# Attention in a fused block kernel: query and key stacks padded with zeros to all 128 rows

## The chip, the cores and the metric

The kernel runs on one core of a Trainium2 chip, in one launch. The metric is the device time of that launch in microseconds (us), as the median of several runs; less is better. A further execution is recorded by the hardware profiler. Engines are named as in the profile: PE multiplies matrices (PEld is its weight load), DVE, ACT and POOL work on vectors, SP issues most of the DMA transfers. "PEclk" is the share of its full clock that TensorE was granted. L1104 is line 1104 of the kernel before.

## What is computed

Four sequences of 512 tokens with 128 channels pass through four residual blocks: a Mamba block with a mixture of eight experts, a feed-forward block (FFN), causal attention with 16 heads of 8 channels, and the same FFN again. Attention is the part that the change touches:

```python
q = (x @ W_dq.T @ W_uq.T).reshape(B, T, nh, hs)
q_lat = jnp.einsum('bqhd,hdl->bhql', q, k_eff)
attn = jnp.einsum('bhql,bkl->bhqk', q_lat, c_kv) / sqrt(hs)
attn = jnp.where(causal[None, None], attn, -jnp.inf)
attn = jax.nn.softmax(attn, axis=-1)
y_lat = jnp.einsum('bhqk,bkl->bhql', attn, c_kv)
y = jnp.einsum('bhql,hld->bqhd', y_lat, v_eff).reshape(B, T, C)
```

## The kernel before

The first half of the launch runs the Mamba scan of one sequence after another, with routing, experts and FFN of earlier sequences beside it. The second half is attention, again beside what is left of experts, FFN and projections.

**Stacks.** The projection of a sequence (`project`, L500 to L533) splits each fp32 query and key value into three bf16 parts and stores them in DRAM (`q_d` at L528, three copies in `k_d` at L531, both issued by POOL). Attention goes by eight units, a unit being eight heads of a sequence. `fill(u)` (L1079) loads a unit into one of three pairs of stacks, `qs` and `ks`, with six DMAs on SP's queue. A stack has 96 rows: rows 0 to 71 (`NP9`) hold three blocks of 24 rows, arranged so that one bf16 matmul over 72 rows sums the nine products of the parts. Rows 72 to 74 of `ks` hold -1 for good (`below`, written once per stack by the DMA of L1062); rows 72 to 74 of `qs` receive the three bf16 parts of the row maxima.

**Maxima.** `maxima(u)` (L1090) computes all scores of a unit over rows 0 to 71 (L1104), adds the causal mask on the diagonal block by a 128-row matmul with the identity (L1108), and DVE takes the row maximum straight from PSUM (L1100). The maxima are split (L1120 to L1123), transposed (L1127), written to DRAM (`m_d`, L1133) and read back into three rows of `qs` (L1134), both by POOL.

**Exponentials.** `exps(G)` (L1140) takes four heads: it computes the transposed scores over 75 rows (L1157), in which the three extra rows subtract the maximum, adds the mask (L1165), and ACT takes the exponential (L1170). `weigh(G)` (L1173) multiplies the exponentials with the values in fp32, four heads side by side of 32 columns each (`po`, L1184), and transposes the result (L1198).

Per four heads `exps` streams 5,120 columns of scores and 2,048 of masks; `maxima` streams 10,240 and 4,096 per unit.

**Order.** The loop at L1254 interleaves the exponentials of one half unit, the maxima of the next unit, the weighing of the half unit before, and pieces of the experts (L335 to L391), the FFN (L426 to L459) and the projections. Python emits that order, and in this second half a scheduler of the framework then sets each engine's final order by its own estimates of durations, so an edit can move instructions that it does not name. PSUM tiles of scores are double (`sq`, `st`), the general tile `mm` is single.

Of the kernel before, what the change touches and what calls it, by code (L numbers as in the profile page):

```python
# [10 lines left out]
BF16 = mybir.dt.bfloat16  # L11
# [5 lines left out]
P = 128  # L17
B, L, C = 4, 512, 128
# [7 lines left out]
NH, HS, KVL = 16, 8, 64  # L26
# [11 lines left out]
def block_kernel(ctx, tc, x, rms1_w, rms2_w, in_proj_w, conv_w, conv_b, x_proj_w,  # L38
                 dt_proj_w, dt_proj_b, A_log, D_skip, out_proj_w, router_w, Wg, Wu, Wd,
                 W_dq, W_dqT, W_uqT, W_dkvT, W_uk, W_uv, W_oT, w_gateT, w_upT, w_downT, out):  # L40
    nc = tc.nc
    const = ctx.enter_context(tc.tile_pool(name="const", bufs=1))
# [45 lines left out]

    below = const.tile([3, L], BF16, tag="below", name="below")
    nc.gpsimd.memset(below, -1.0)  # L90
    identb = const.tile([P, P], BF16, tag="identb", name="identb")
    nc.vector.tensor_copy(identb, ident)
    maskq = const.tile([P, P], BF16, tag="maskq", name="maskq")
# [92 lines left out]
    rows = [keep.tile([P, NT, 2], I32, tag="rows", name=f"rows{b}") for b in range(B)]  # L186
# [410 lines left out]
    with ExitStack() as first:  # L597
        w1 = first.enter_context(tc.tile_pool(name="s1", bufs=1))
# [6 lines left out]
        h0, xi, sz, dt, bc, c_d, delta, du = {}, {}, {}, {}, {}, {}, {}, {}  # L605
# [430 lines left out]
    with ExitStack() as second:  # L1036
        def pool(name, bufs, **more):
            return second.enter_context(
                tc.tile_pool(name=name, bufs=bufs, reuse_waits="tile", **more)
            )  # L1040

        w1, w2 = pool("a1", 1), pool("a2", 2)
# [9 lines left out]

        NP9 = 9 * HS
        NU = NH // 2
        UNITS = 2 * B
        qs, ks = [], []
        for i in range(3):
            qs.append(w1.tile([96, NU, L], BF16, tag=f"qs{i}", name=f"qs{i}"))  # L1060
            k = w1.tile([96, NU, L], BF16, tag=f"ks{i}", name=f"ks{i}")
            nc.sync.dma_start(  # L1062
                k[NP9 : NP9 + 3, :, :], below.unsqueeze(1).to_broadcast([3, NU, L])
            )
            ks.append(k)

        def values(b):
            va, qk = vs[b % 2], stores[b][2]
# [10 lines left out]
        def fill(u):  # L1079

            b, h0 = u // 2, (u % 2) * NU
            q_d, k_d, _ = stores[b]
            for i in range(3):
                at = slice(3 * HS * i, 3 * HS * (i + 1))
                for stack, of in ((qs[u % 3], q_d), (ks[u % 3], k_d[i])):
                    nc.sync.dma_start(
                        stack[at], of[:, :, h0 : h0 + NU, :].rearrange("j d h l -> (j d) h l")
                    )

        def maxima(u):  # L1090

            q, k = qs[u % 3], ks[u % 3]
            mx = w2.tile([P, NT, NU], F32, tag="mx", name="mx")
            taken = None
            for t in range(NT):
                w = (t + 1) * P
                n = L // w
                for h0 in range(0, NU, n):
                    if taken:
                        nc.vector.tensor_reduce(*taken, AX.X, ALU.max)  # L1100
                    sc = ps_q.tile([P, L], F32, tag="sq", name="sc")
                    for h in range(h0, h0 + n):
                        c = (h - h0) * w
                        nc.tensor.matmul(  # L1104
                            sc[:, c : c + w], q[0:NP9, h, t * P : w], k[0:NP9, h, 0:w],
                            start=(h == h0), stop=False, skip_group_check=True,
                        )
                    nc.tensor.matmul(  # L1108
                        sc[:, 0 : n * w].rearrange("p (h k) -> p h k", k=w)[:, :, t * P : w],
                        identb, maskq.unsqueeze(1).to_broadcast([P, n, P]),  # L1110
                        start=False, stop=True, skip_group_check=True,
                    )
                    taken = (
                        mx[:, t, h0 : h0 + n], sc[:, 0 : n * w].rearrange("p (h k) -> p h k", k=w)
                    )
                    yield
            nc.vector.tensor_reduce(*taken, AX.X, ALU.max)
            parts = w2.tile([P, NT, 3, NU], BF16, tag="mparts", name="mparts")
            rest = w2.tile([P, NT, NU], F32, tag="mrest", name="mrest")
            nc.vector.tensor_copy(parts[:, :, 0, :], mx)  # L1120
            nc.vector.tensor_tensor(rest, mx, parts[:, :, 0, :], ALU.subtract)
            nc.vector.tensor_copy(parts[:, :, 1, :], rest)
            nc.vector.tensor_tensor(parts[:, :, 2, :], rest, parts[:, :, 1, :], ALU.subtract)  # L1123
            yield
            pm = ps.tile([3 * NU, L], BF16, tag="mm", name="pmx")
            for t in range(NT):
                nc.tensor.transpose(  # L1127
                    pm[:, t * P : (t + 1) * P], parts[:, t].rearrange("p i h -> p (i h)"), identb
                )
            mT = w2.tile([3 * NU, L], BF16, tag="mT", name="mT")  # L1130
            nc.scalar.copy(mT, pm)  # L1131
            m_d = dram.tile([3, NU, L], BF16, tag="m_d", name="m_d")
            nc.gpsimd.dma_start(m_d.rearrange("i h l -> (i h) l"), mT)  # L1133
            nc.gpsimd.dma_start(q[NP9 : NP9 + 3, :, :], m_d)  # L1134
            yield

        scale = float(HS) ** -0.5
# [2 lines left out]
        def exps(G):  # L1140


            u, h0 = G // 2, 4 * (G % 2)
            q, k = qs[u % 3], ks[u % 3]
            probs[G] = got = [{} for _ in range(4)]

            for blocks in (
                [(0, 0, 0)], [(1, 0, 0)], [(2, 0, 0)], [(3, 0, 0)],
                [(0, 1, 0), (0, 3, L - P)], [(1, 1, 0), (1, 3, L - P)],
                [(2, 1, 0), (2, 3, L - P)], [(3, 1, 0), (3, 3, L - P)],  # L1150
                [(0, 2, 0), (1, 2, 2 * P)], [(2, 2, 0), (3, 2, 2 * P)],
            ):
                pt = ps_t.tile([P, L], F32, tag="st", name="st")
                p = w2.tile([P, L], F32, tag="p", name="p", bufs=PBUFS)
                for j, kt, c in blocks:
                    rows = slice(kt * P, (kt + 1) * P)
                    nc.tensor.matmul(  # L1157
                        pt[:, c : c + L - kt * P], k[0 : NP9 + 3, h0 + j, rows],
                        q[0 : NP9 + 3, h0 + j, kt * P : L],
                        start=(c == 0), stop=False, skip_group_check=True,  # L1160
                    )
                    got[j][kt] = p[:, c : c + L - kt * P]

                n, step = len(blocks), blocks[-1][2] // P or 1
                nc.tensor.matmul(  # L1165
                    pt.rearrange("p (a c) -> p a c", c=P)[:, 0 : step * (n - 1) + 1 : step, :],
                    identb, maskk.unsqueeze(1).to_broadcast([P, n, P]),
                    start=False, stop=True, skip_group_check=True,
                )
                ready[G] = nc.scalar.activation(p, pt, AF.Exp, scale=scale).ins  # L1170
                yield
# [74 lines left out]
        while 0 not in stores:  # L1246
            turn(*streams)
        fill(0)
        fill(1)
        for _ in range(2):  # L1250
            turn(*streams)
        for _ in times(2, maxima(0)):
            turn(*streams)
        for G in range(2 * UNITS + 1):  # L1254
            u = G // 2
            if G % 2 == 0:
                ends.add(*(last(b) for b in begin.get(u, ())))
                while filled < min(u + 3, UNITS) and filled // 2 in stores:
                    fill(filled)
                    filled += 1  # L1260
                if u < UNITS and u % 2 == 0:
                    values(u // 2)
                while u + 1 < UNITS and filled <= u + 1:
                    turn(*streams)
                    if filled // 2 in stores:
                        fill(filled)
                        filled += 1
                more = maxima(u + 1) if u + 1 < UNITS else iter(())
            scores = exps(G) if G < 2 * UNITS else iter(())
            weighed = weigh(G - 1) if 1 <= G else iter(())  # L1270
            for step in range(10):
# [74 lines left out]
```

## Time and profile before

| what | value |
|---|---|
| median of 3 runs | 939.68 us (939.14 to 942.08) |
| the profiled execution | 941.45 us, of which its span is 939.6 us |
| mean granted clock of TensorE | 0.854 |
| PE, DVE, ACT, POOL busy | 734.1, 580.3, 411.2, 309.4 us |
| bytes moved by DMA | 99.16 MB, 106 GB/s over the span |
| first and last matmul of L1104 | 470.4 and 872.8 us from the span's start |
| first and last matmul of L1157 | 525.6 and 901.9 us |

In a group's row, "72\*128 72x384 bf16" means 72 rows and 128 columns of the array in use and a moving operand of 72 partitions by 384 elements; then follow the count, the busy time with the mean in ns of one, and the idle time of the engine just before, with what ended it. A row of a view by stretches has the stretch, its length, each engine's busy time with the number of instructions begun, the granted clock, the share of the DMA engines and their rate.

### The profile page before, as it was taken

The page shows a single profiled execution, that of the slowest core. Times are in us where ns is not written, and L with a number is a line of the kernel's source. Part 1 is how long each engine was busy: PE and PEld are TensorE (multiplying, and loading weights), DVE is VectorE, ACT ScalarE, POOL GpSimd, SP SyncE. Part 2 cuts the span into 40 slices and gives each one's busy share as a digit, 9 for nine tenths or more (in the row PEclk, how much of TensorE's full clock was granted, in tenths as well). Part 3 has the DMA queues.
Part 4 walks back from the last instruction along what each step waited for, and adds up shares of the span by engine and source line. Part 5 has one row for each costly group of instructions (what it writes and reads, how often), then busy time and mean ns, then how long its engine had stood idle before and what let it go on. Part 6 is the DMA issues. An engine that isn't in the chain of part 4 may idle for free. (4 is left out here: it accounts for less than half of the span.)

```text
span 939.6 us, 11943 instructions
## 1 busy us (share of the span) xinstructions
PE 734.1 (78%) x3763; PEld 429.0 (46%) x3763; DVE 580.3 (62%) x1151; ACT 411.2 (44%) x794; POOL 309.4 (33%) x243
## 2 busy tenths in 40 slices
PE   5386698689879865788398799789858997889854
PEld 2132243255356621557357476458724454355432
DVE  4395999899989898747274552166544156566311
ACT  2836548535854431324103354503345533554641
POOL 1153664856556348432402104000161402300010
PEclk9688789789989977799759599979968897997987
DMA  4138221163157412516546235817410330600000
GB/s 103 35 140 325 65 68 47 53 194 112 64 171 233 132 46 82 172 46 202 178 125 204 80 117 168 211 45 220 143 43 3 93 87 7 163 16 3 3 12 11
DMA packets 84480, 99.16 MB, mean 106 GB/s; under 512 B 10370, under 2 KB 56458, under 8 KB 83242
## 3 DMA queue, kind: packets, MB, share of 16 engines
q1 hardware_dynamic: 78881, 87.09, 31.3%
q0 software_dynamic: 4352, 10.89, 3.6%
q10 hardware_dynamic: 1184, 0.43, 0.2%
q8 instruction: 30, 0.49, 0.2%
q14 instruction: 33, 0.26, 0.1%
HBM read 76.67 MB, written 21.63 MB: 105 GB/s over the span
## 5 line engine op out<-in xcount | busy, mean ns | idle before, releaser
L886 POOL TENSOR_TENSOR hc<-hst,cs 128x1024 f32<-128x1024 f32 x64 | 150.6, 2353 | 138.7 <-issue 34.3
L832 PE MATMUL yp<-hc,ident 128*128 128x512 f32 x256 | 150.6, 718 | 43.6 <-POOL hc L886 42.5
L874 DVE TENSOR_TENSOR_SCAN hst<-da,bx 128x1024 f32<-128x1024 f32 x64 | 146.3, 2286 | 10.7 <-POOL hc L886 3.7
L1100 DVE TENSOR_REDUCE mx<-sc 128x1 f32<-128x384 f32 (+3 forms) x168 | 102.7, 636 | 66.4 <-PE sc L1108 64.8
L832 PEld LDWEIGHTS yp<-hc,ident 128*128 128x128 f32 x256 | 52.7, 220 | 140.6 <-POOL hc L886 98.9
L1170 ACT ACTIVATE p<-st 128x512 f32<-128x512 f32 x160 | 90.9, 598 | 34.3 <-PE st L1165 31.0
L812 ACT ACTIVATE da<-delta,A 128x512 f32<-128x512 f32 (+1 forms) x128 | 84.7, 715 | 41.1 <-DVE hst L874 38.5
L1104 PE MATMUL sc<-ks,qs 72*128 72x128 bf16 (+3 forms) x256 | 76.7, 358 | 15.5 <-DMA ks<-k_d 8.2
L854 DVE TENSOR_TENSOR bx<-du,pb 128x1024 f32<-128x1024 f32 x64 | 78.3, 1223 | 5.0 <-POOL du L803 2.5
L319 DVE SCALAR_TENSOR_TENSOR thm<-thm,mpg 128x512 f32<-128x512 f32 x53 | 36.1, 680 | 70.4 <-ACT thm L380 70.4
L374 PE MATMUL mpg<-xTm,wgu 128*128 128x128 f32 x424 | 67.1, 301 | 11.1 <-DMA wgu<-in_Wg_dram 6.7
L1157 PE MATMUL st<-qs,ks 75*128 75x512 bf16 (+3 forms) x256 | 67.7, 331 | 10.3 <-ACT p L1170 5.6
L374 PEld LDWEIGHTS mpg<-xTm,wgu 128*128 128x128 f32 x424 | 60.3, 214 | 20.3 <-issue 8.4
L374 PE MATMUL mpu<-xTm,wgu 128*128 128x128 f32 x424 | 62.2, 292 | 5.8 <-DVE mh L320 4.1
L1133 POOL DMA_DIRECT2D m_d<-mT x8 | 4.4, 550 | 184.3 <-ACT mT L1131 184.3
L367 ACT ACTIVATE xTm<-mpt,r2w 128x128 f32<-128x128 f32 x53 | 19.4, 366 | 102.9 <-PE mpt L365 102.9
L386 PE MATMUL mpd<-wd,mh 128*128 128x128 f32 x424 | 60.2, 286 | 2.8 <-ACT xTm L367 2.3
L374 PEld LDWEIGHTS mpu<-xTm,wgu 128*128 128x128 f32 x424 | 57.3, 209 | 8.7 <-DVE mh L320 4.4
L822 PE MATMUL pb<-bc,pick 96*128 96x512 bf16 x64 | 27.4, 429 | 41.8 <-DVE bx L854 38.0
L386 PEld LDWEIGHTS mpd<-wd,mh 128*128 128x128 f32 x424 | 53.4, 197 | 7.0 <-ACT xTm L367 5.3
L1108 PE MATMUL sc<-maskq,identb 128*128 128x128 bf16 (+2 forms) x176 | 50.1, 284 | 0.0
L380 ACT ACTIVATE thm<-mpg 128x512 f32<-128x512 f32 x53 | 31.7, 597 | 40.9 <-PE mpg L374 39.9
(242 smaller groups left out, 1167.1 us busy)
## 6 DMA issues: line engine op xcount, KB each, us to landing
cs<-c_d SPq DMA_DIRECT2D x64, 256.0 KB
wgu<-in_Wg_dram SPq DMA_DIRECT2D x53, 256.0 KB
wgu<-in_Wu_dram SPq DMA_DIRECT2D x53, 256.0 KB
wd<-in_Wd_dram SPq DMA_DIRECT2D x53, 256.0 KB
xg<-zero SPq DMA_DIRECT2D x8, 1024.0 KB
qs<-q_d SPq DMA_DIRECT2D x24, 192.0 KB
k_d<-parts POOLq DMA_DIRECT2D x12, 384.0 KB, 4.0
ks<-k_d SPq DMA_DIRECT2D x24, 192.0 KB
```

What stands on the lines that cost most here:

```text
L374: nc.tensor.matmul(pp[:, f, :], w[:, k, f * P : (f + 1) * P], rows_in, start=True, stop=True,)
L386: nc.tensor.matmul(pd, hT[:, f, :], w[:, f, :], start=(f == 0), stop=(f == NFC - 1))
L812: nc.scalar.activation(da[:, e, e:], delta[b][:, e, e:], AF.Exp, scale=A[:, e, n : n + 1])
L832: nc.tensor.matmul(yps[b][:, e, :], ident, hc[:, e, :], start=(n == 0), stop=(n == NS - 1))
L854: nc.vector.tensor_tensor(bxs[s], du[s // NS], taps[s][1].unsqueeze(1).to_broadcast([P, NE, L]), ALU.mult)
L874: nc.vector.tensor_tensor_scan(hst.rearrange("p e l -> p (e l)"), dec.pop(s).rearrange("p e l -> p (e l)"), bxs.pop(s).rearrange("p e l -> ...
L886: done = nc.gpsimd.tensor_tensor(hc, hst, cs.unsqueeze(1).to_broadcast([P, NE, L]), ALU.mult).ins
L1100: nc.vector.tensor_reduce(*taken, AX.X, ALU.max)
L1104: nc.tensor.matmul(sc[:, c : c + w], q[0:NP9, h, t * P : w], k[0:NP9, h, 0:w], start=(h == h0), stop=False, skip_group_check=True,)
L1108: nc.tensor.matmul(sc[:, 0 : n * w].rearrange("p (h k) -> p h k", k=w)[:, :, t * P : w], identb, maskq.unsqueeze(1).to_broadcast([P, n, P] ...
L1157: nc.tensor.matmul(pt[:, c : c + L - kt * P], k[0 : NP9 + 3, h0 + j, rows], q[0 : NP9 + 3, h0 + j, kt * P : L], start=(c == 0), stop=False ...
L1170: ready[G] = nc.scalar.activation(p, pt, AF.Exp, scale=scale).ins
```

## The change

Both stacks get 128 rows. Rows 0 to 71 stay as they are, rows 72 to 124 are zeros in both, and the rows of the maxima and of -1 move to 125 to 127. The matmuls of the maxima then run over 125 rows, those of the exponentials over 128. The zeros come from a new constant `blank` of 53 partitions by 512, set once by POOL; when each of the three pairs is filled for the first time (units 0, 1 and 2), two DMAs on SP's queue copy it eight times over into `qs` and `ks` (53 x 8 x 512 bf16, 434 KB each). The DMA of `below` moves from the set-up to the same place.

```diff
+    blank = const.tile([P - 3 - 9 * HS, L], BF16, tag="blank", name="blank")
+    nc.gpsimd.memset(blank, 0.0)
...
-        NP9 = 9 * HS
+        NP9, MXR = 9 * HS, P - 3
...
-            qs.append(w1.tile([96, NU, L], BF16, tag=f"qs{i}", name=f"qs{i}"))
-            k = w1.tile([96, NU, L], BF16, tag=f"ks{i}", name=f"ks{i}")
-            nc.sync.dma_start(
-                k[NP9 : NP9 + 3, :, :], below.unsqueeze(1).to_broadcast([3, NU, L])
-            )
-            ks.append(k)
+            qs.append(w1.tile([P, NU, L], BF16, tag=f"qs{i}", name=f"qs{i}"))
+            ks.append(w1.tile([P, NU, L], BF16, tag=f"ks{i}", name=f"ks{i}"))
...
+            if u < 3:
+                for stack in (qs[u], ks[u]):
+                    nc.sync.dma_start(
+                        stack[NP9:MXR], blank.unsqueeze(1).to_broadcast([MXR - NP9, NU, L])
+                    )
+                nc.sync.dma_start(ks[u][MXR:P], below.unsqueeze(1).to_broadcast([3, NU, L]))
...
-                            sc[:, c : c + w], q[0:NP9, h, t * P : w], k[0:NP9, h, 0:w],
+                            sc[:, c : c + w], q[0:MXR, h, t * P : w], k[0:MXR, h, 0:w],
...
-            nc.gpsimd.dma_start(q[NP9 : NP9 + 3, :, :], m_d)
+            nc.gpsimd.dma_start(q[MXR:P, :, :], m_d)
...
-                        pt[:, c : c + L - kt * P], k[0 : NP9 + 3, h0 + j, rows],
-                        q[0 : NP9 + 3, h0 + j, kt * P : L],
+                        pt[:, c : c + L - kt * P], k[:, h0 + j, rows],
+                        q[:, h0 + j, kt * P : L],
```

In the built program PE, DVE and ACT have the same instructions as before, POOL has one more (the setting of `blank`) and SP six more DMAs. On SP the fills of `qs` and `ks` of unit 0 stand where the three DMAs of `below` stood; the fill of unit 1's `qs` stands just ahead of an expert's weight loads and of the first load of `q_d`; the fill of unit 1's `ks` stands between the six loads of unit 0 and those of unit 1; both fills of unit 2 stand some 80 places ahead of unit 2's loads. The scheduler also orders PE anew in two stretches: between the maxima of units 0 and 2, and in the stretch of experts beside unit 2's maxima. From the scores of the second sequence to the end PE's order is the same, but for one pair of exponential and maxima steps.

## The prediction

> **What bounds the kernel.** I read the page's slices first. From slice 20 on (470 us) attention runs, and PE is the fullest engine by far; but the clock row shows that it is often not granted its full clock while it is full.
>
> ```profile
> PE   5386698689879865788398799789858997889854
> ...
> PEclk9688789789989977799759599979968897997987
> ```
>
> So I asked for stretches of low clock with PE busy (columns: PE, PEld, DVE, ACT, POOL busy, then the clock):
>
> ```profile
> core 0: us, PE busy (x) PEld busy (x) DVE busy (x) ACT busy (x) POOL busy (x), PEclk, DMA share, GB/s
> 470.40:488.00 17.60, 16.24 (x65) 7.92 (x65) 14.61 (x27) 0.37 (x1) 0.00 (x0) 0.50 0.61 159
> 525.20:538.00 12.80, 12.80 (x55) 7.09 (x52) 7.75 (x21) 7.60 (x15) 0.00 (x0) 0.50 0.12 43
> 538.00:541.00 3.00, 3.00 (x34) 1.04 (x34) 0.20 (x1) 0.80 (x2) 0.00 (x0) 0.77 0.00 0
> 621.30:634.90 13.60, 12.72 (x52) 8.43 (x52) 9.36 (x18) 0.96 (x2) 0.00 (x0) 0.50 0.00 0
> ...
> 720.30:737.30 17.00, 15.16 (x37) 6.01 (x36) 6.18 (x49) 11.35 (x23) 2.97 (x4) 0.60 0.00 0
> 771.50:778.30 6.80, 6.04 (x21) 2.38 (x19) 5.90 (x11) 0.00 (x0) 0.00 (x0) 0.50 0.01 2
> 856.80:866.10 9.30, 9.24 (x41) 4.90 (x38) 5.95 (x16) 5.89 (x11) 1.13 (x1) 0.50 0.01 2
> 866.10:870.50 4.40, 4.40 (x33) 1.38 (x32) 2.25 (x15) 0.28 (x1) 0.00 (x0) 0.50 0.00 0
> ```
>
> From 525 to 538 us PE has no gap at all and still gets half its clock. These stretches hold the score matmuls; they end when 128-row fp32 matmuls of experts, FFN or `po` come. The next view sets two full stretches against each other, PE alone: scores and masks, then experts, and what follows the experts.
>
> ```profile
> core 0: us, PE busy (x), PEclk, DMA share, GB/s
> 529.10:532.50 3.40, 3.40 (x17) 0.50 0.01 2
> 532.50:535.90 3.40, 3.40 (x17) 0.50 0.00 0
> 631.50:634.90 3.40, 3.40 (x18) 0.50 0.00 0
> 635.00:638.40 3.40, 3.40 (x30) 1.00 0.37 101
> ```
>
> **What sets the clock.** The Trainium skill ("TensorE: Matmul & The Clock Gate", Part 1, The HAM clock gate) says that the clock follows how busy PE has been, and opens after one busy window of about 3.4 us. The changes of clock in this trace do lie on a grid of 3.41 us. But 12.80 us busy of 12.80 at clock 0.50 contradicts the rest: busy time alone is not what counts. I laid the trace's matmuls on that grid and counted streamed columns, fp32 twice, each weighted by rows in use over 128 and columns in use over 128, against what half the clock could stream. Of 80 windows at half clock, the 53 that stayed there reach at most 0.74, the 27 that opened have at least 0.75: no overlap. Without the weight by rows, a window with 1.00 stays shut and one with 0.79 opens. At full clock, the clock falls when about 0.36 of the full capacity is no longer reached (28 falls, none above 0.40; 162 stay, none under 0.33). From the code, a PE full of `exps` reaches (5120 x 75/128 + 2048) / 7168 = 0.70, full of `maxima` (10240 x 72/128 + 4096) / 14336 = 0.69: under 0.75 however full it is. After the change these are 1.00 and 0.98. The masks count in full although their identity and most of their mask are zeros (leaving them out, 3 of 80 windows go wrong), so I take zero rows to count. By the skill's rule the change gains nothing and costs what its DMAs cost; by the trace it opens the clock. I follow the trace.
>
> **The matmuls themselves.** 256 + 256 matmuls get more rows. Weight loads show no cost of rows: 115 and 108 ns with 72 and 75 rows, 108 ns with 128.
>
> ```profile
> L1104 PEld LDWEIGHTS <-qs 72*128 72x128 bf16 x256 | 27.8, 115 | 31.4 <-issue 26.4
> L1157 PEld LDWEIGHTS <-ks 75*128 75x128 bf16 x256 | 27.2, 108 | 29.0 <-issue 21.7
> L1108 PEld LDWEIGHTS <-identb 128*128 128x128 bf16 x176 | 18.9, 108 | 16.6 <-issue 12.9
> ```
>
> Matmuls at one clock are as long as their columns: nothing here.
>
> **What the clock gives, stretch by stretch.** A stretch at full clock can't be shorter than half its PE time, nor than its DVE or ACT time; nor do these overlap fully. The same sequence of steps as at 856.0 to 866.1 (10.10 us) runs at full clock in 792.8 to 800.4, 7.60 us, with ACT busy 5.93 of it (0.78) and with two projection matmuls of 1.06 us together that the other lacks. So I divide the largest of the three by about 0.85, and `po` goes from 4.43 to about 2.35 us:
>
> ```profile
> 847.96 2.29 PE po L1184 x32
> 866.17 4.43 PE po L1184 x32
> ```
>
> - 470.4 to 488 (first maxima): DVE is busy 14.61 of 17.60, so it binds (in the same loop at full clock, 616 to 620, it was busy 3.99 of 4). Up to 2.5, less the first window, cold after idle, and the start: 1. Then experts start at full clock instead of cold until 491.6: about 1. Together 2.0.
> - 525.2 to 541: the first 3.9 us stay cold after idle. The remaining 8.9 us hold 5.4 of DVE and 5.3 of ACT, over 0.85 is 6.3: 2.6; `po` 0.6. Together 3.2.
> - 621.3 to 634.9: DVE binds until 628 (0.2), then cold experts fill PE for 6.8 us: half would be 3.4, I take 2.8. Together 3.0.
> - 682.7 to 689.6, the same pattern: 0, since the FFN behind it waits for POOL's gathers of expert rows until 700 us anyway.
> - 720.3 to 737.3: ACT 11.35 / 0.85 = 13.4, so 3.6; but projection matmuls with 64 rows in it can still shut the clock: 2.5.
> - 771.5 to 778.3: DVE 5.90 binds: 0.4.
> - 856.8 to 870.5: between 9.30 - 5.95 / 0.85 = 2.3 and 10.10 - (7.60 - 1.06) = 3.6, take 2.2; `po` 2.0. Together 4.2.
>
> Sum: 15.3 us. Bounds: with DVE and ACT no limit it would be about 30; with the clock shutting again where DVE binds (there a window weighs only about 0.38 to 0.40 at full clock, close to the 0.36 of the falls), 7.
>
> **The DMAs.** Six fills of 424 packets of 1 KB. The 1 KB packets of `below` took 82 ns each, so a fill is 424 x 82 / 16 = 2.2 us of all DMA engines if spread evenly, up to twice that if not, and 0.8 to 1.4 us of SP (`below` 0.78, the zero fill of the experts' rows 1.39). Unit 0's two run in 409 to 423 us, where DMA was idle (1 GB/s at 410 to 412): 0. Unit 2's two come near 543 us, with DMA nearly idle until 555: 0. The fill of unit 1's `ks` stands behind the load that PE waits for (second row below) and ahead of unit 1's loads, not used before 492; weight loads behind it land 2.2 us later, against experts at 488: 0 to 1, take 0.5. The fill of unit 1's `qs` comes near 446 us, where ACT waits for the store of `q_d` and PE behind it (first row):
>
> ```profile
> PE mpt L365 <- ACT full L523: 7.2, 1, 7.2
> PE sc L1104 <- DMA ks<-k_d: 8.2, 1, 8.2
> ```
>
> 0 to 4.4, take 1.0, as the store is on another queue and starts at 448. The setting of `blank` on POOL costs 0.5 us at 3 us, ahead of nothing used before 11 us: 0. The moved `below` DMAs ride with the fills. The new order of PE between 492 and 600 us: -2 to +2, take 0.
>
> **Sum.** -15.3 + 1.5 = -13.8 us, against the profiled 941.45: 927.7. The median stands 1.8 under that execution: 939.7 - 13.8 = 925.9.
>
> **Rivals.** A measurement of this kernel can tell about 0.3% (2.8 us) from no change.
> - *The clock opens as said* (0.60): 925.9, own range 916 to 932.
> - *It opens, but waits take most of it* (0.18): DVE and ACT bind nearer to 1.0, and windows near 0.36 shut again. For: DVE 14.61 of 17.60 and ACT 11.35 of 17.00. Against: `po` and experts bind on PE alone, 7 us. -7 + 1.5: 934.
> - *Zero rows don't count, or a weight I took for rows is one for bf16* (0.10): the change doesn't do what it says. For: the score matmuls are also nearly the only bf16 ones; a weight of 0.7 for bf16 misplaces just 3 windows of 80. Then +1.5: 941.
> - *Slower* (0.12): the same shut clock, and the fills lie on the path: unit 1's `qs` fill holds up the store of `q_d` (4.4 if uneven) and unit 1's `ks` fill the weights at 488 (up to 2.2). It decides if the clock stays 0.50 in the first exponentials and PE's wait for `full` exceeds 9 us: 945.
>
> Faster by over 0.3%: 0.78; within: 0.10; slower: 0.12. The range runs from the 916 of the first case to 941, which takes in the second and most of the third.
>
> **What would show it.** Right: clock 1.0 from one window after the first `exps` starts, mean clock near 0.88, `po` never at 4.4 us, L1104 and L1157 means well under 358 and 331 ns, PE's wait before the first L1104 still near 8 us. Wrong: a PE full of 128-row scores at 0.50 for over two windows; or a clock that is open with the time unchanged, and DVE or ACT waits longer by as much.

## The result and the profile after

The changed kernel takes 993.05 us (median of 4 runs, 991.29 to 998.51), the kernel before 940.88 beside it: a ratio of 1.056 (95% interval 1.052 to 1.061). The profiled execution took 993.71 us with a span of 991.9. The forecast was 925.9, and 993 lies far outside its range of 916 to 941. Medians are over all runs of a kernel and ratios over those within 1.5% of its fastest, which matters for the kernel before, 938.2 over 39 runs and 934.6 over 21 in the first of the three sets below, and for `rows80`, 935.6 over 20 and 930.1 over 11.

In the changed kernel the scores are L1109, their mask L1113, the exponentials' scores L1162, `po` L1189, the experts' first product L377; the fills are L1084 (`blank`) and L1087 (`below`), the loads of the stacks L1091. Two rows of the slices and three of the groups from the page of the changed kernel, then the same three groups before:

```profile
PE   5396697699798757836356890888985887979964
...
PEclk9687798799999767868577795899997998989997
...
L377 PE MATMUL mpg<-xTm,wgu 128*128 128x128 f32 x424 | 70.2, 310 | 59.7 <-DMA wgu<-in_Wg_dram 58.8
...
L1109 PE MATMUL sc<-ks,qs 125*128 125x128 bf16 (+3 forms) x256 | 65.6, 313 | 28.9 <-DMA yg<-ym 14.1
...
L1162 PE MATMUL st<-qs,ks 128*128 128x128 bf16 (+3 forms) x247 | 58.8, 299 | 13.4 <-ACT p L1175 6.8
```

```profile
L1104 PE MATMUL sc<-ks,qs 72*128 72x128 bf16 (+3 forms) x256 | 76.7, 358 | 15.5 <-DMA ks<-k_d 8.2
...
L374 PE MATMUL mpg<-xTm,wgu 128*128 128x128 f32 x424 | 67.1, 301 | 11.1 <-DMA wgu<-in_Wg_dram 6.7
L1157 PE MATMUL st<-qs,ks 75*128 75x512 bf16 (+3 forms) x256 | 67.7, 331 | 10.3 <-ACT p L1170 5.6
```

The score matmuls did get shorter, 358 to 313 ns and 331 to 299 ns in the mean: the clock opened for part of them. But PE has holes (counted from 1, a 3 in slice 18, 3, 5 and 6 in slices 20 to 22, a 0 in slice 25), and 58.8 us of them stand ahead of the experts' first product, which waits for its weights; before, that was 6.7 us. The weights are loaded by SP's queue, so the next view is SP's own timeline (start, duration, instruction), cut to the fills and to issues of over 10 us:

```profile
406.02 0.88 SPq L1084 DMA_DIRECT2D qs<-blank  x1
406.95 14.70 SPq L1084 DMA_DIRECT2D ks<-blank  x1
421.70 18.10 SPq L1087 DMA_DIRECT2D ks<-below  x1
...
464.69 0.72 SPq L1084 DMA_DIRECT2D qs<-blank  x1
465.86 17.58 SPq L360 DMA_DIRECT2D wgu<-in_Wg_dram  x1
...
495.56 0.70 SPq L1084 DMA_DIRECT2D ks<-blank  x1
496.30 17.67 SPq L1087 DMA_DIRECT2D ks<-below  x1
...
578.59 0.78 SPq L1084 DMA_DIRECT2D qs<-blank  x1
579.48 14.35 SPq L348 DMA_DIRECT2D yg<-ym  x1
...
596.38 0.71 SPq L1084 DMA_DIRECT2D ks<-blank  x1
597.13 16.23 SPq L1087 DMA_DIRECT2D ks<-below  x1
```

The issue of a fill takes under 1 us when nothing is ahead of it, and the issue behind it, which needs 0.3 to 0.8 us as a rule, takes 14 to 18 us. Six fills, six such holds, 98.6 us of SP together. What the DMA engines do meanwhile, in 40 slices of 406 to 440 us (busy tenths of 16 engines, GB/s), and over 420 to 440 us:

```profile
DMA  7840000000000000000100000000000000000000
GB/s 274 254 125 17 24 24 24 24 24 24 24 24 23 24 23 24 23 24 24 42 34 23 24 23 24 23 24 23 24 23 24 23 24 23 24 23 24 24 23 24
```

```profile
core 0: us, PE busy (x) PEld busy (x) DVE busy (x) ACT busy (x) POOL busy (x), PEclk, DMA share, GB/s
420.00:440.00 20.00, 8.59 (x66) 7.62 (x66) 7.77 (x38) 6.49 (x18) 1.28 (x1) 0.77 0.07 25
```

They are all but idle: 24 GB/s for 30 us. A share of 0.07 is 1.1 of 16 engines. In the trace the 1 KB packets of a fill last 46 ns each and start 43 ns apart, never more than two at a time. So a fill of 424 packets runs on one DMA engine and takes 424 KiB / 24 GB/s = 18 us. PE meanwhile (waits from 400 to 520 us, then from 520 to 700; total, times, longest):

```profile
PE mpg L377 <- DMA wgu<-in_Wg_dram: 27.7, 2, 17.4
PE mpt L368 <- ACT full L526: 11.2, 1, 11.2
```

```profile
PE mpg L377 <- DMA wgu<-in_Wg_dram: 30.7, 4, 28.0
PE sc L1109 <- DMA yg<-ym: 14.1, 1, 14.1
```

From 600 to 620 us PE does nothing at all:

```profile
core 0: us, PE busy (x) PEld busy (x) DVE busy (x) ACT busy (x) POOL busy (x), PEclk, DMA share, GB/s
600.00:620.00 20.00, 0.00 (x0) 0.00 (x0) 0.00 (x0) 1.49 (x4) 0.00 (x0) 0.50 0.24 70
```

**Theory.** The number of rows of a fill, 53, is prime, and so one DMA engine gets all of it; the queue that issued it is held for about as long, and every load behind it is late. The clock gives what was forecast. **Rivals:** the traffic of the fills is dear in itself, however it is spread; the 125-row matmuls or the new order of PE's instructions cost; the zeros don't open the clock, something else in the change does.

### The profile page after: what moved, and what is told of

It is laid out like the page before. It is cut to its first block, busy times and chain, and to the rows that moved or that the text cites. A ratio compares the mean times of both kernels' runs of the same rounds, so it can differ in the third digit from the quotient of the medians.

```text
span 991.9 us, 11930 instructions
## 1 busy us (share of the span) xinstructions
PE 718.6 (72%) x3754; PEld 426.6 (43%) x3763; DVE 578.5 (58%) x1151; ACT 410.1 (41%) x794; POOL 310.5 (31%) x244
## 5 line engine op out<-in xcount | busy, mean ns | idle before, releaser
L377 PE MATMUL mpg<-xTm,wgu 128*128 128x128 f32 x424 | 70.2, 310 | 59.7 <-DMA wgu<-in_Wg_dram 58.8
L377 PEld LDWEIGHTS mpg<-xTm,wgu 128*128 128x128 f32 x424 | 63.3, 222 | 70.8 <-issue 63.9
L1109 PE MATMUL sc<-ks,qs 125*128 125x128 bf16 (+3 forms) x256 | 65.6, 313 | 28.9 <-DMA yg<-ym 14.1
L1162 PE MATMUL st<-qs,ks 128*128 128x128 bf16 (+3 forms) x247 | 58.8, 299 | 13.4 <-ACT p L1175 6.8
L389 PE MATMUL mpd<-wd,mh 128*128 128x128 f32 x424 | 62.2, 289 | 2.9 <-ACT xTm L370 2.1
L377 PE MATMUL mpu<-xTm,wgu 128*128 128x128 f32 x424 | 64.2, 297 | 0.0
L377 PEld LDWEIGHTS mpu<-xTm,wgu 128*128 128x128 f32 x424 | 59.3, 214 | 3.2 <-issue 1.7
L261 POOL DMA_INDIRECT xg<-hs,rows x32 | 32.4, 1012 | 45.7 <-DVE rows L253 38.4
```

What stands on the lines that cost most here:

```text
L377: nc.tensor.matmul(pp[:, f, :], w[:, k, f * P : (f + 1) * P], rows_in, start=True, stop=True,)
L389: nc.tensor.matmul(pd, hT[:, f, :], w[:, f, :], start=(f == 0), stop=(f == NFC - 1))
L1109: nc.tensor.matmul(sc[:, c : c + w], q[0:MXR, h, t * P : w], k[0:MXR, h, 0:w], start=(h == h0), stop=False, skip_group_check=True,)
L1162: nc.tensor.matmul(pt[:, c : c + L - kt * P], k[:, h0 + j, rows], q[:, h0 + j, kt * P : L], start=(c == 0), stop=False, skip_group_check=True,
```

## The experiments

None leaves out a part of the computation. The kernel before stood at 938.2, 939.1 and 939.3 us beside the three sets (`split48_5` to `rows127_fill52`; `rows80` to `zeros_by_pool`; the last three). In the built programs, PE's order is the same in the changed kernel, `fills_only`, `rows127_fill52`, `rows80` and `fill56_52` (here: order A); one DMA more per fill gives another order (B: `split48_5`, `split_fills_only`, `rows96`, `fill52_1`, `fill51_2`). `fills_on_pool` and `zeros_by_pool` have orders of their own.

### Each fill in two pieces, all rows kept: split48_5

```diff
-                    nc.sync.dma_start(
-                        stack[NP9:MXR], blank.unsqueeze(1).to_broadcast([MXR - NP9, NU, L])
-                    )
+                    for lo, n in ((NP9, 48), (NP9 + 48, 5)):
+                        nc.sync.dma_start(
+                            stack[lo : lo + n], blank[0:n].unsqueeze(1).to_broadcast([n, NU, L])
+                        )
```

> The changed kernel, but each zero fill of 53 rows is issued as two DMAs, of 48 and of 5 rows; same bytes, same packets of 1 KB. One-engine theory (a DMA of 53 rows runs on one DMA engine, because 53 has no divisor up to 16, and its full ring holds up SP's queue): no fill holds SP for over 2 us, PE's waits for expert weights fall back to about the 7 us of before, the open clock is what remains: 920 to 932 us. Bytes theory (2.6 MB more in small packets crowd out the weights): as the changed kernel, 985 to 995. Rows theory (125 and 128 rows cost time in the matmuls): above 970.

925.75 us (20 runs, 922.34 to 930.42), ratio 0.993 (0.990 to 0.996). The same bytes in the same places, 67 us less than the changed kernel: it is not the traffic, but how a fill is spread. The longest entry of a fill on SP is 3.3 us, for two of them, and one issue of `below` behind them takes 3.3 us; I had expected no more than 2.

### The fills without the rows, whole and in pieces: fills_only, split_fills_only

The zeros go to rows 75 to 127, which no matmul reads; scores stay at 72 and 75 rows.

```diff
-                        stack[NP9:MXR], blank.unsqueeze(1).to_broadcast([MXR - NP9, NU, L])
+                        stack[NP9 + 3 : P], blank.unsqueeze(1).to_broadcast([MXR - NP9, NU, L])
...
-                            sc[:, c : c + w], q[0:MXR, h, t * P : w], k[0:MXR, h, 0:w],
+                            sc[:, c : c + w], q[0:NP9, h, t * P : w], k[0:NP9, h, 0:w],
...
-                        pt[:, c : c + L - kt * P], k[:, h0 + j, rows],
-                        q[:, h0 + j, kt * P : L],
+                        pt[:, c : c + L - kt * P], k[0 : NP9 + 3, h0 + j, rows],
+                        q[0 : NP9 + 3, h0 + j, kt * P : L],
```

> The six fills of 53 rows go into rows 75 to 127, which no matmul reads; the matmuls keep 72 and 75 rows and the maxima rows 72 to 74. One-engine theory: the whole delay and none of the clock, 1000 to 1015 us, with SP held for about 100 us in all. Rows theory: about 940.

1008.32 us (1005.44 to 1012.16), ratio 1.079 (1.069 to 1.089), mean clock 0.822. The fills make the loss without the rows, and SP is held as in the changed kernel (14.4 to 18.4 us, six times).

> As the run with the fills alone, matmuls of 72 and 75 rows, but the fills as 48 and 5 rows. One-engine theory: 939 to 944 us, the fills cost next to nothing and the clock stays as before. Bytes theory: about 1005. Against the run with split fills and full rows this gives what the rows do to the clock: forecast 12 to 18 us.

935.44 us (20 runs, 927.62 to 943.18), ratio 0.999 (0.996 to 1.001). Fills in pieces cost nothing that can be measured; I had expected 939 to 944. Against `split48_5`, which has the same order and the same fills but the full rows, 9.7 us are the rows' own gain, under the 12 to 18 that I had expected; against `fill52_1` below, of the same order too, it is 15.9.

### One row fewer, 52 rows a fill: rows127_fill52

```diff
-        NP9, MXR = 9 * HS, P - 3
+        NP9, MXR = 9 * HS, P - 4
```

(with `blank` one row shorter, and the maxima in rows 124 to 126)

> The changed kernel with one zero row less: stacks of 127 rows, fills of 52 rows in one DMA each, maxima in rows 124 to 126. Bytes fall by 2% only. One-engine theory: 52 divides by 13, so 13 engines share a fill (about 2.7 us instead of 18), SP isn't held, 920 to 934 us. Bytes theory and rows theory: 985 to 995.

916.50 us (915.27 to 920.15), ratio 0.982 (0.974 to 0.991). One row less in a fill takes 76.5 us from the changed kernel, in the very same order of PE's instructions, and stands 3.5 us under the range that I expected.

### Fewer rows of zeros: rows80, rows96

The stack ends at row 80 or 96; the matmuls read 77 and 80, or 93 and 96 rows; the fills have 5 rows, or 16 and 5.

```diff
-        NP9, MXR = 9 * HS, P - 3
+        NP9, MXR = 9 * HS, 80 - 3
...
-                        stack[NP9:MXR], blank.unsqueeze(1).to_broadcast([MXR - NP9, NU, L])
+                            stack[lo : lo + n], blank[0:n].unsqueeze(1).to_broadcast([n, NU, L])
```

> The stack ends at row 80: only 5 rows of zeros, so each fill is 5 rows of 8 KB (40 KB) and is no longer in anybody's way, and the score matmuls read 77 and 80 rows. Clock by rows in use: the exponentials' and maxima's stretches then stand near 0.73 and 0.71 of the half clock's columns, below the 0.75 at which windows opened before, so the clock stays shut there as before: 934 to 941 us, level with the kernel before and with the one that only splits fills. If what opens the clock is something else that the zero rows bring (the fills' own traffic, the shifted order of work), 80 rows give it too: about 926.

935.56 us (20 runs, 923.48 to 942.55), ratio 0.993 (0.990 to 0.997): as I had expected by the median of all runs, some us better by the runs that the ratio counts.

> The stack ends at row 96: 21 rows of zeros, filled as 16 and 5 rows, and the score matmuls read 93 and 96 rows. Clock by rows in use: 0.82 and 0.79 of the half clock's columns where 0.75 opened windows, so most of the gain is there: 920 to 930 us. If the array counts activity in strips of 32 rows, 72 to 96 rows are one and the same, and the time is that of the kernel before and of 80 rows: 934 to 941. If only a full array opens the clock: the same 934 to 941.

930.61 us (929.12 to 931.64), ratio 0.988 (0.982 to 0.994). The granted clock from 465 us to the end of the span:

| rows in the score matmuls | kernel | mean clock |
|---|---|---|
| 72 and 75 | before; `split_fills_only` | 0.84; 0.84 |
| 77 and 80 | `rows80` | 0.84 |
| 93 and 96 | `rows96` | 0.86 |
| 125 and 128 | `split48_5`; `fill52_1`; `fill56_52` | 0.90; 0.92; 0.92 |

80 rows leave the clock as it was, and 96 rows bring only a part: of the three kernels of one order, `rows96` has 4.8 us of the 9.7 (`split48_5`) or 15.9 (`fill52_1`). It goes by rows, not by "full or not" nor by the fills' presence. But 930.6 lies just over the range that I expected, and the trace shows one reason: I had weighed only the opening of the clock, not its falling. The maxima of a unit at full clock, by 3.4 us, with 96 rows and then with 128 (`fill56_52`, below):

```profile
core 0: us, PE busy (x) PEld busy (x) DVE busy (x) ACT busy (x) POOL busy (x), PEclk, DMA share, GB/s
758.20:761.60 3.40, 3.35 (x30) 2.89 (x29) 3.13 (x5) 0.54 (x2) 0.00 (x0) 1.00 0.00 0
761.60:765.00 3.40, 2.39 (x13) 1.26 (x13) 3.38 (x8) 0.30 (x1) 1.26 (x1) 1.00 0.00 0
765.00:768.40 3.40, 3.16 (x11) 1.26 (x10) 2.93 (x6) 0.00 (x0) 0.00 (x0) 0.50 0.00 0
768.40:771.80 3.40, 3.05 (x10) 1.01 (x8) 3.05 (x5) 0.00 (x0) 0.00 (x0) 0.50 0.02 5
```

```profile
core 0: us, PE busy (x) PEld busy (x) DVE busy (x) ACT busy (x) POOL busy (x), PEclk, DMA share, GB/s
750.60:754.00 3.40, 2.60 (x14) 1.33 (x14) 3.38 (x7) 0.00 (x0) 0.83 (x1) 1.00 0.00 0
754.00:757.40 3.40, 2.46 (x13) 1.10 (x12) 3.39 (x7) 0.00 (x0) 0.00 (x0) 1.00 0.02 5
```

In both DVE is full (3.38 of 3.40), so PE streams little more than 0.4 of its capacity in such windows. Weighted by 93 of 128 rows, the window from 761.6 us comes to about 0.3 and the clock falls behind it; with 125 rows the two windows come to over 0.4 and the clock stays. How much of the missing gain such falls make up was not measured.

### The fills on another queue: fills_on_pool

```diff
-                    nc.sync.dma_start(
+                    nc.gpsimd.dma_start(
                         stack[NP9:MXR], blank.unsqueeze(1).to_broadcast([MXR - NP9, NU, L])
```

> The changed kernel, but its fills of 53 rows leave SyncE's queue for GpSimd's; the fills of three rows stay on SyncE. If the 67 us are SyncE's queue being held while one DMA engine takes a fill of 18 us (the loads of weights wait behind it), then most of it comes back: 925 to 950 us, with no issue of SyncE's above a few us for a load of weights, and the fills themselves still some 18 us long. If the slow fill itself is what the products of the stacks wait for, or if the full DMA engine delays the weights' own share on it, it stays near 990.

987.17 us (984.18 to 991.84), ratio 1.048 (1.041 to 1.056). I expected SP to come free, and it does: from 395 to 640 us no issue of SP's is longer than 6.0 us. PE's wait for weights (L377, from 400 to 700 us) falls with it, from 58.4 to 14.6 us. But the time stays. POOL's queue now has the fills, each 31.5 to 33.2 us from issue to landing in the median, and POOL stores `q_d` and gathers the experts' rows. From POOL's timeline (the idle time before an instruction, and what ended it, in brackets):

```profile
452.49 3.09 POOL L1084 DMA_DIRECT2D ks<-blank  x1 [2.59 <-issue]
480.45 3.09 POOL L1084 DMA_DIRECT2D qs<-blank  x1 [24.88 <-issue]
486.04 3.08 POOL L1084 DMA_DIRECT2D ks<-blank  x1 [2.50 <-issue]
...
512.24 0.97 POOL L261 DMA_INDIRECT xg<-hs,rows  x1 [13.10 <-DMA qs<-blank]
```

and of ACT's waits from 440 to 540 us

```profile
ACT parts L525 <- DMA q_d<-parts: 50.3, 1, 50.3
```

Before, that wait was 6.3 us. The weights come in time again although the fills are no faster, which speaks for the held queue of SP and against the busy engine as what kept them; what stands behind the fills on POOL is late instead, and costs as much. It is no proof, since this kernel has orders of its own.

### No fill by DMA: zeros_by_pool

```diff
-                    nc.sync.dma_start(
-                        stack[NP9:MXR], blank.unsqueeze(1).to_broadcast([MXR - NP9, NU, L])
-                    )
+                    nc.gpsimd.memset(stack[P // 2 : P], 0.0)
```

> The changed kernel with no fill by DMA for the zeros: GpSimd writes zeros into rows 64 to 127 of each stack of products (eight heads by 512 columns) before the products are copied in. By the theory of the fills (one DMA engine, held queue) the loss is gone: 916 to 932 us, as with the fills split. If the copies into the stacks come to wait for GpSimd (a memset of 4096 columns of bf16 may take several us, before each of the stacks), it is up to 10 us more, and the products' copies wait on POOL in the trace.

937.0 us (20 runs, 929.6 to 941.69), ratio 0.997 (0.995 to 1.000): 5 us over the first range that I expected, within the 10 more of the second, but not by the copies' waiting for POOL. The holds are gone, but the first score matmul comes at 490.4 us, 21 us later than in `split48_5`, after a delay that I had not thought of. POOL's and then DVE's timeline:

```profile
434.06 3.53 POOL L1081 MEMSET qs<- 64x4096 bf16 x1
437.53 3.53 POOL L1081 MEMSET ks<- 64x4096 bf16 x1
```

```profile
434.17 3.44 DVE L136 TENSOR_SCALAR rs_t<-ln_v 128x4 int32<-128x4 int32 x1
437.65 3.44 DVE L139 TENSOR_SCALAR rs_r<-rs_t 128x4 int32<-128x4 int32 x1
441.12 0.16 DVE L143 TENSOR_TENSOR rs_t<-rs_r 128x4 f32<-128x4 f32 x1
```

Two instructions on 4 elements a row last as long as POOL's settings beside them; in `split48_5` the same two took 0.17 and 0.16 us. All five of DVE's TENSOR_SCALAR that begin during one of the six settings end with it, some 14 us of delay together, while other instructions of DVE beside the settings keep their time (SCALAR_TENSOR_TENSOR on 128x512, 0.69 us). Behind them on DVE stand the routing's steps, for which POOL's gathers wait: the first gather comes at 460.3 us, in `split48_5` at 438.3. That these 14 us make up most of the 21 is likely but was not tried, as this kernel has orders of its own.

### How many engines a fill gets: fill52_1, fill51_2, fill56_52

The first two split the fill as in `split48_5`, as 52 and 1 or as 51 and 2 rows:

```diff
-                    for lo, n in ((NP9, 48), (NP9 + 48, 5)):
+                    for lo, n in ((NP9, 51), (NP9 + 51, 2)):
```

> The same with 51 rows and 2 rows: 51 is 3 times 17, so if a fill takes the largest divisor of its rows up to 16 as its number of DMA engines, this one runs on 3 of them: 408 KB at three times the 24 GB/s of one engine, 5.7 us a fill instead of 18, and issues on SyncE that are held for a few us or not at all. Of the 67 us that 53 rows cost, each of six fills being held some 15 us, a part below a third stays: 928 to 950 us. If only a fill on one engine is slow and three are as good as sixteen: 926, with fills of 1 to 2 us. If all odd numbers of rows run on one engine: about 990.

935.97 us (20 runs, 930.13 to 940.41), ratio 0.998 (0.995 to 1.000). From its view by stretches, while fills run, and from SP's timeline (two issues in each entry):

```profile
core 0: us, PE busy (x) PEld busy (x) DVE busy (x) ACT busy (x) POOL busy (x), PEclk, DMA share, GB/s
410.00:412.00 2.00, 2.00 (x17) 1.79 (x16) 0.21 (x1) 0.00 (x0) 0.00 (x0) 1.00 0.20 61
...
470.00:473.00 3.00, 2.94 (x16) 1.72 (x16) 1.86 (x3) 0.00 (x0) 0.00 (x0) 0.50 0.20 66
```

```profile
463.98 5.99 SPq L1085 DMA_DIRECT2D qs<-blank  x2
470.01 6.99 SPq L1085 DMA_DIRECT2D ks<-blank  x2
```

61 to 66 GB/s at a DMA share of 0.20, 3.2 engines of 16, where 53 rows had 24 GB/s; and holds of 6 and 7 us for two issues.

> The change with each fill as 52 rows and 1 row: the fill's speed is that of the 127-row kernel's 52 rows, but there are two fills for one, as in the kernel that splits 48 and 5, whose order of TensorE's instructions it has too. If the 9 us between those two kernels come from the order that one more DMA per stack gives, it stays near 926 us (922 to 930); if they come from the speed of a 48-row against a 52-row fill or the traffic of the short piece, it goes to 916 to 920.

919.56 us (918.25 to 921.12), ratio 0.980 (0.975 to 0.984). This is the second case of what I expected. With 51 rows instead of 52, 16.4 us more. It also fells the thought that order B is slower than order A: this kernel has order B, is level with `fill56_52` of order A (below), and is 6.2 us faster than `split48_5`.

> The change as it is (125 and 128 rows, TensorE's instructions in the very order of the changed kernel), only no fill has 53 rows: the queries' stack is filled in 56 rows (72 to 127, the last three are written again by the maxima), the keys' in 52, and the constant rows are four (124 to 127; the fourth meets a row of zeros). If the number of rows decides how many DMA engines share a fill, 56 and 52 rows take about 1.5 us instead of 18, no issue on SyncE is held, and the time is that of the 127-row kernel, which has the same order: 914 to 920 us, some 75 below the changed kernel. If the 127-row kernel owes its lead over the split fills (916.5 against 925.8) to its rows and not to the order: about 925.

```diff
-                for stack in (qs[u], ks[u]):
+                for stack, n in ((qs[u], 56), (ks[u], 52)):
                     nc.sync.dma_start(
-                        stack[NP9:MXR], blank.unsqueeze(1).to_broadcast([MXR - NP9, NU, L])
+                        stack[NP9 : NP9 + n], blank[0:n].unsqueeze(1).to_broadcast([n, NU, L])
                     )
-                nc.sync.dma_start(ks[u][MXR:P], below.unsqueeze(1).to_broadcast([3, NU, L]))
+                nc.sync.dma_start(ks[u][MXR - 1 : P], below.unsqueeze(1).to_broadcast([4, NU, L]))
```

918.01 us (6 runs, 916.69 to 922.07), ratio 0.979 (0.975 to 0.982). This is the change itself, rows and order and all, with other numbers of rows in its fills: 2.1% faster than the kernel before (1.8 to 2.5%), and level with `rows127_fill52`. Its two fills of unit 0 run at about 170 to 200 GB/s (404 to 414 us in 40 slices, then one stretch of it):

```profile
GB/s 139 221 197 328 238 279 401 352 328 346 316 242 195 213 213 184 193 176 184 184 172 180 180 172 168 168 164 164 164 168 164 123 53 37 33 20 21 0 0 0
```

```profile
408.00:409.00 1.00, 0.00 (x0) 0.00 (x0) 0.63 (x1) 0.00 (x0) 1.00 (x1) 1.00 0.83 184
```

A share of 0.83 is 13.3 engines of 16. The rate doesn't grow with their number: 184 GB/s are some 14 an engine, against 24 for one engine alone, and a 1 KB packet lasts 72 ns in the median, not 46. In `split48_5`, where 48 rows and their pieces keep all 16 busy (407 to 409.8 us, share 1.04), it is 141 GB/s.

Two stretches with exponentials, in the place of those that the prediction shows at 0.60 (720 us) and 0.50 (857 us):

```profile
705.00:722.00 17.00, 13.81 (x47) 5.51 (x45) 5.66 (x31) 11.31 (x25) 3.74 (x5) 1.00 0.10 29
...
840.00:855.00 15.00, 13.95 (x127) 7.35 (x128) 9.97 (x35) 11.57 (x24) 0.93 (x2) 1.00 0.02 3
```

## Why the prediction was wrong

The four kernels of order A make a rough square (medians, us); its first row sets 72 and 75 rows beside 77 and 80:

| | fills on one engine | fills spread | price of the fills |
|---|---|---|---|
| 72 to 80 rows | 1008.3 (`fills_only`) | 935.6 (`rows80`) | 72.8 |
| 125 and 128 rows | 993.05 (the change) | 918.0 (`fill56_52`) | 75.0 |
| gain of the rows | 15.3 | 17.5 | |

The kernel before stood at 938.2 to 940.9 beside them. The price of the fills is far outside all spread. The gain of the rows is softer: over the runs that its ratio counts, `rows80` stands at 930.1, and the 17.5 become 12.1; in order B the rows give 9.7 or 15.9. From 939.3 before, the new order of PE and five more rows with cheap fills give -3.7, the other rows -17.5, the fills on one engine +75.0, together 993.1; with 930.1 for `rows80` the first two are -9.2 and -12.1, so how their sum of -21.3 divides is not settled.

**The step that failed** is in the part on the DMAs: "a fill is 424 x 82 / 16 = 2.2 us of all DMA engines if spread evenly, up to twice that if not". The upper bound was no bound: "not even" can mean one engine of sixteen, and then a fill takes 18 us. The same sentence gave each fill "0.8 to 1.4 us of SP"; SP was held 14 to 18 us behind each. The number for an even spread was good: two fills of 54 rows on average went at some 180 GB/s in `fill56_52`, 2.5 us each. The 82 ns packets of `below` that I scaled say nothing of how many engines a transfer of 53 rows gets. But the trace before had a warning: the three DMAs of `below`, 3 rows each, ran with a DMA share of 0.15, 2.4 of 16 engines, and 26 GB/s.

```profile
408.00:410.00 2.00, 0.17 (x1) 0.17 (x1) 0.81 (x2) 0.00 (x0) 1.78 (x1) 0.92 0.15 26
```

The Trainium skill states the rule that was missing ("DMA: Bandwidth & Descriptors", section "Why a DMA increments its semaphore by 16 and not by 1"): a transfer is shared by the largest number of engines up to 16 that divides the slowest dimension longer than 1 of both its patterns. For 53 that is 1, for 51 it is 3, for 52 it is 13, for 56 it is 14. The runs agree: 1.1 engines busy and 24 GB/s for 53 rows, 3.2 and 61 to 66 GB/s for 51, 13.3 and 184 GB/s for 56 and 52.

**From that the zeros in the list of fills were wrong too.** "Unit 0's two ... 0", "unit 2's two ... 0": idle DMA engines are no cover for a transfer that uses one of them, and neither line thought of what stands behind the fill on SP's queue: the next fill and `below`, then the loads for the experts. The changed kernel against `fill56_52`, which differ in the fills alone, by milestones (start, us; `po` is counted from the first of L1189):

| | changed | fill56_52 | late | fills since the line above |
|---|---|---|---|---|
| first L1109 | 501.1 | 471.1 | 30.0 | both of unit 0, `qs` of unit 1 |
| first `po` | 571.7 | 524.9 | 46.8 | `ks` of unit 1 |
| second `po` | 637.2 | 560.8 | 76.4 | both of unit 2 |
| end | 991.9 | 915.3 | 76.6 | none |

Nothing is caught up, and 98.6 us of holds became 76.6. The forecast had 1.5 here.

**The rival "slower" (945)** had the right place, the fills on the path, with the weights and the store of `q_d` behind them, and the right sign; its price was bound by the same 4.4 and 2.2 us. Of the two signs that were to decide it, one came: PE's wait for `full` was 11.2 us, over 9. The other, a clock that stays shut, did not: the first exponentials start at 565.1 us, and from 560 to 598 us the clock is 1.00. Nor does the loss need it: `fills_only` has the same holds.

**The clock part held, in mechanism and size.** 15.3 us were forecast for the rows, 10 to 17.5 measured. That one of the pairs gives 15.3 again is luck, for by place it was less right. `fills_only` against the changed kernel, which have the same order and the same fills (spans 1008.4 and 991.9):

| until | forecast | gained since the line above |
|---|---|---|
| fourth `po` (the first maxima and exponentials) | 5.2 | 1.0 |
| fifth `po` (experts beside maxima) | 3.0 | 6.9 |
| seventh `po` (720 to 737 before) | 2.5 | 2.7 |
| ninth `po` (771 to 778 before) | 0.4 | 1.9 |
| end | 4.2 | 3.9 |

Two things stand behind the first line. The slow fills hide the gain: in 506 to 518 us the changed kernel does the work of the first maxima in 6.24 us of PE where `fills_only` takes 9.98, but then both wait for weights and have PE busy 1.38 and 1.24 of 12 us until 530. And "the new order of PE between 492 and 600 us: -2 to +2, take 0" left out that the order mixes experts, which use all rows, into the first exponentials: the clock is 0.90 in 558 to 571 us in `fills_only` already. The third rival, that zero rows don't count, is out: `rows80` to `fill56_52` differ in rows of zeros, with the same order and type, and gain 12 to 17.5 us. The second rival's worry, windows at 0.36 to 0.40 that shut the clock again, is seen at 96 rows; with 125 and 128 the two windows shown stayed open. As for the signs named ahead, the mean clock was 0.855 and not 0.88, with 0.50 while PE stood idle (600 to 620 us), and one `po` still took 4.0 us.

**Weights.** "Weight loads show no cost of rows": the loads of L1104 last 99 ns in the median, those of L1109 98. "Matmuls at one clock are as long as their columns" was given without a number: the shortest score matmuls of 128, 256, 384 and 512 columns take 217, 269, 322 and 376 ns with 72 rows, and 216, 269, 322 and 376 with 125. Both terms of nothing were right.

**Open.** `split48_5` is 6.2 us slower than `fill52_1`, with the same order and bytes. It begins in the first maxima (468 to 490 us): its clock stays at 0.50 there, with windows at about 0.6 to 0.75 of the half clock's capacity, while in `fill52_1` a window of about 0.84 opens it at 476. What keeps PE below is not settled. The edges themselves are not sharp. If each matmul's columns are laid on the grid from its start on, the 80 windows and 28 falls of the kernel before are the same, but a window of 0.73 opens and one of 0.75 stays shut, and falls reach up to 0.37 while windows stay open from 0.29; over the other kernels openings and shut windows overlap between 0.72 and 0.79. So "no overlap" hung on how the matmuls were laid; the weight by rows did not, as without it windows of 1.00 stay shut. And why SP is held was not tried by itself; that the issue behind a fill waits for about as long as the fill lasts is what the timeline shows. The forecast also took 0.3% for what a measurement can tell; the kernel before ranged from 928.1 to 948.0 us in 38 runs.

## What to carry to other kernels

Before a DMA is costed at bytes over bandwidth, factor its outermost count: 53 rows, a prime above 16, put it on one engine (24 GB/s here), and the price was paid by whatever stood behind it on the queue that issued it; a row less, a few more, or a piece cut off took 67 to 77 us from this kernel, unless it left three engines (57). Padding a matmul with rows of zeros is a way to open TensorE's clock where PE is full and still gets half of it (here 10 to 17.5 us, 1.0 to 1.9%), but it must carry the windows in which another engine binds over the point at which the clock falls, not only those in which PE is full. When an edit joins a cheap helper to a main idea, run the helper alone first: `fills_only`, at 1008.3 us, shows the whole loss.

## What the runs showed of the hardware that I had not expected

- A DMA of 53 rows by 8 KB: 24 GB/s, 18 us, and the issue behind it held 14 to 18 us on SP. More engines each move less: 24 GB/s with one, 61 to 66 with three, 184 with 13, 141 with all 16 (48 rows and pieces of 5).
- Two small DVE instructions lasted 3.44 us each beside POOL's settings of 64 x 4096 bf16 (3.53 us), instead of 0.17: a TENSOR_SCALAR of DVE was stopped for as long as one POOL instruction lasted, a SCALAR_TENSOR_TENSOR was not.
- The granted clock counts rows that hold zeros: from 465 us on it is 0.84 in the mean with 77 and 80 rows in use, 0.86 with 93 and 96, 0.90 to 0.92 with 125 and 128.
- In 20 runs each, kernels with 72 to 80 rows spread over 16 to 19 us (`split_fills_only`, `rows80`), kernels with 125 and 128 over 8 to 12 (`split48_5`, `fill51_2`, `zeros_by_pool`); why was not tried.
